# Turning image tokens by 32x32 blocks and transfers inside SBUF in place of TensorE's transposes

## The chip, the cores and the metric

The kernel runs on one core of one Trainium2 chip. A core has TensorE (PE: matrix products, and transposes as a product with a unit matrix), VectorE (DVE), ScalarE (ACT), GpSimd (POOL) and SyncE (SP, which here only issues transfers), with SBUF and PSUM as its memories on chip; 16 DMA engines move data. The metric is device time in microseconds.

## The reference, cut to what matters

The input `x` is an image of 256 channels and 48 x 48 points. Layer 0 normalises it by groups, makes queries, keys and values of 4 heads of 64 and lets all 4 x 2304 = 9216 rows attend to each other; the result, projected, is added to `x`. Layer 1 takes the image as 2304 tokens of 256 channels, adds an attention over 64 learned slices, and then a mixture of 8 experts, of which each token uses two.

```python
qf = q.reshape(B*H*W*nh, dk) / sqrt(dk)          # 9216 x 64
A = softmax(qf @ kf.T, axis=1)                   # 9216 x 9216
x = x + transpose(((A @ vf).reshape(B,H,W,nh*dv)) @ Wo.T + bo)
t = tokens(x)                                    # channels x points  ->  points x channels
h = _ln_t(t) @ W0 + b0                           # normalised over a token's channels
sw = softmax(h @ Ws + bs)                        # 64 slice weights of each token
# slice sums of tokens (weights sw), attention over slices, back to the tokens, then the experts
```

What the change touches is the step `tokens(x)`: the kernel holds `x` with the channels on the partitions, and needs it with the points on the partitions as well.

## The kernel before, in words

Everything is float32. The first 65 us load the image and weights, normalise, and make keys `kk`, queries `q2` and values `v_sb`. The attention of layer 0 then runs to about 1217 us; what follows (the slices' attention, the routing, the experts) ends at 1591.5.

*The attention.* `attention` (L527) runs 18 blocks `b` of 512 queries, two for each group `g` of 256 points (two tiles of 128 points), and in each block 36 pairs of key tiles. For a pair, `scores` makes four products of 64x64 tiles into PSUM (`s`, two buffers), ScalarE takes the exponential into `p` (five buffers), `sums` adds `p` to `acc` on VectorE, and `times_values`, one pair later in TensorE's order, makes four products into `av`, which has one buffer for the whole block. At a block's end `close` (L606) folds `av` into `up` on VectorE; the next block's first `av` product can't start before that has been read.

*The order.* The engines' instructions are recorded through `InOrder` (L52), which keeps them in the written order: each engine works through its own list and waits at its head. TensorE's side work for earlier groups stands at the second pair of a block (`between`, `follow`). The other engines' side work is a list `later`: each piece has a rank, the list is sorted by it (`in_turn`, L417), and one piece is taken from it after the sum of each pair. The ranks give an order and no time.

*The side work.* Group g's blocks are b = 2g and 2g + 1. In block 2g + 3 stands `out_proj` (L421): the output projection into a PSUM bank `pa` and its addition to `x_sb` on VectorE (two pieces). In block 2g + 4 stands `slices` (L439): TensorE transposes the group's four 128x128 pieces of `x_sb` into `pa` and makes the slice and gate logits into `pb`. From `pa` VectorE takes mean and variance of each token (`spread`: `bn_stats`, `bn_aggr`), ScalarE copies the tokens to `t_sb` (`keep`), GpSimd raises the variance to -1/2 (`scales`), and VectorE later writes the normalised tokens `tn` (`norm`). `logits`, `exps`, `gates`, `weights` make the slice weights `sw` from `pb`. In block 2g + 6 stands `gather` (L507): TensorE sums the normalised tokens by slice weights, and VectorE adds the result to `sums_of`. In the last block the side work of groups 6 and 7 that is left is drained in two further steps, each issued once the list before it is empty. The ninth group, g = 8, follows after the attention.

SP issues nothing between the loads at the start and the experts' weights after the attention.

Of the kernel before, what the change touches and what calls it, by code (L numbers as in the profile page):

```python
# [9 lines left out]
FP = mybir.dt.float32  # L10
AF = mybir.ActivationFunctionType
ALU = mybir.AluOpType
# [3 lines left out]
P = 128  # L16
C = 256
# [5 lines left out]
TG = 256  # L23
# [23 lines left out]
def bc(ap, shape):  # L47

    return ap.unsqueeze(2).to_broadcast(shape)
# [16 lines left out]
def layers(  # L66
# [10 lines left out]
    nc = tc.nc  # L77
# [3 lines left out]
    pe, dve, act, pool = (InOrder(tc, e) for e in (nc.tensor, nc.vector, nc.scalar, nc.gpsimd))  # L81
    small = ctx.enter_context(tc.tile_pool(name="small", bufs=2))
# [8 lines left out]
        out=gmat, in_=gmat, pattern=[[-8, 16], [0, 8]], compare_op=ALU.is_ge,  # L91
# [3 lines left out]
        out=gmat, in_=gmat, pattern=[[8, 16], [0, 8]], compare_op=ALU.is_ge,  # L95
        fill=0.0, base=7, channel_multiplier=-1,
    )
    mhalf = const.tile([P, NTT], FP, name="mhalf")
# [11 lines left out]
        out=not_before, in_=not_before, pattern=[[-1, P]], compare_op=ALU.is_ge,  # L110
# [32 lines left out]
    stats = const.tile([P, NTT, 2], FP, name="stats")  # L143
    rstd_t = const.tile([P, NTT], FP, name="rstd_t")
# [10 lines left out]
    t_sb = const.tile([P, NTT, C + E], FP, name="t_sb")  # L155
# [4 lines left out]
    x_sb = l0.tile([P, 2, NT], FP, name="x_sb")  # L160
    for c, pieces in enumerate(((1152, 1152), (1152, 768, 384))):
        at = 0
# [48 lines left out]
    for h in range(H1):  # L211
        at = ((h // 2) % 2 * 2 + h // 4) * D1
        nc.sync.dma_start(
            out=Wout_sb[at : at + D1, h % 2, 0:C], in_=Wout[h * D1 : (h + 1) * D1, :]
# [24 lines left out]
    with proj, tc.tile_pool(name="ps_pj", bufs=5, space=PSUM) as ps_pj, tc.tile_pool(  # L239
        name="ps_spun", bufs=1, space=PSUM  # L240
    ) as ps_spun, tc.tile_pool(
        name="ps_w", bufs=2, space=PSUM
# [49 lines left out]
        for bi, (t0, tn) in enumerate(TBLOCKS):  # L292
            toks = slice(t0, t0 + tn)
# [5 lines left out]
            for m in range(2):  # L299
# [11 lines left out]
                for j in range(2):  # L311
                    rows = slice(j * DK, (j + 1) * DK)
                    at = (2 * m + j) * NT + t0
# [97 lines left out]
    side = layer0.enter_context(tc.tile_pool(name="side", bufs=1))  # L411
    OT = side.tile([P, 2, 2, TG], FP, name="OT")
    tn = side.tile([P, 4, C + 1], FP, name="tn")
    dve.memset(tn[:, :, C : C + 1], 1.0)
    NG = NTT // 2

    def in_turn(work):  # L417
# [3 lines left out]
    def out_proj(g, ps, _):  # L421

        toks = slice(g * TG, (g + 1) * TG)
        for m in range(2):
            for c in range(2):
                pe.matmul(
                    ps[:, m * TG : (m + 1) * TG], WoT[:, c, m * P : (m + 1) * P], OT[:, g % 2, c, :],
                    start=(c == 0), stop=(c == 1),
                )

        def add(m):
            dve.scalar_tensor_tensor(
                x_sb[:, m, toks], ps[:, m * TG : (m + 1) * TG], bcol[:, B_O + m : B_O + m + 1],
                x_sb[:, m, toks], ALU.add, ALU.add,
            )

        return [(2, lambda: add(0)), (3, lambda: add(1))]

    def slices(g, ps, pl):  # L439

        two = range(2 * g, 2 * g + 2)
        for c in range(2):
            for u, i in enumerate(two):
                pe.transpose(
                    ps[:, u * C + c * P : u * C + (c + 1) * P], x_sb[:, c, i * P : (i + 1) * P], ident
                )
        for u, i in enumerate(two):
            at = u * (S + E)
            for c in range(2):
                pe.matmul(  # L450
                    pl[:, at : at + P], x_sb[:, c, i * P : (i + 1) * P],
                    Wl_flat[:, c * (S + E) : c * (S + E) + P], start=(c == 0), stop=(c == 1),
                )
        both = pl[:, 0 : 2 * (S + E)].rearrange("p (u s) -> p u s", u=2)
        lg = small.tile([P, 2, S], FP, name="lg", tag="lg")
        sm = small.tile([P, 2], FP, name="sm", tag="sm")
        nm = small.tile([P, 2], FP, name="nm", tag="nm")
        these = slice(2 * g, 2 * g + 2)

        def keep(u):  # L460
            act.copy(t_sb[:, 2 * g + u, 0:C], ps[:, u * C : (u + 1) * C])

        def spread(u):
            s6 = small.tile([P, 6], FP, name="s6", tag="s6")
            dve.bn_stats(s6, ps[:, u * C : (u + 1) * C])
            dve.bn_aggr(stats[:, 2 * g + u, :], s6)

        def scales():
            ve = small.tile([P, 2], FP, name="ve", tag="ve")
            dve.tensor_scalar(ve, stats[:, these, 1], 1e-5, None, ALU.add)  # L470
            pool.tensor_tensor(rstd_t[:, these], ve, mhalf[:, 0:2], ALU.pow)

        def logits():
            for u, i in enumerate(two):
                dve.scalar_tensor_tensor(
                    lg[:, u, :], both[:, u, 0:S], rstd_t[:, i : i + 1], bl_bc, ALU.mult, ALU.add
                )
            dve.tensor_reduce(nm, lg, AX.X, ALU.max, negate=True)

        def exps():  # L480
            for u in range(2):
                act.activation(
                    lg[:, u, :], lg[:, u, :], AF.Exp, bias=nm[:, u : u + 1], accum_out=sm[:, u : u + 1]
                )

        def gates():
            dve.tensor_copy(t_sb[:, these, C : C + E], both[:, :, S : S + E])

        def weights():
            dve.reciprocal(sm, sm)  # L490
            dve.tensor_tensor(sw[:, these, :], lg, bc(sm, [P, 2, S]), ALU.mult)

        def norm(u):
            i = 2 * g + u
            dve.tensor_scalar(
                tn[:, i % 4, 0:C], t_sb[:, i, 0:C], stats[:, i, 0:1], rstd_t[:, i : i + 1],
                ALU.subtract, ALU.mult,
            )

        at = 9 if g == NG - 1 else 16  # L500
        return [
            (2, lambda: spread(0)), (3, lambda: spread(1)), (4, lambda: keep(0)), (5, lambda: keep(1)),
            (6, scales), (8, logits), (9, exps), (10, gates), (11, weights),
            (at, lambda: norm(0)), (at, lambda: norm(1)),
        ]

    def gather(g, _, pl):  # L507

# [7 lines left out]
        def add():  # L516
            if g == 0:
                dve.tensor_copy(sums_of, new)
            else:
                dve.tensor_tensor(sums_of, sums_of, new, ALU.add)  # L520
            if g == NG - 2:
                dve.tensor_scalar(fold_den, fold[:, 1, :], sums_of[:, C : C + 1], None, ALU.mult)
# [4 lines left out]
    def attention():  # L527


        with tc.tile_pool(name="pexp", bufs=5) as pexp, tc.tile_pool(  # L530
# [104 lines left out]
            def follow(k):  # L635

                pa = ps_side.tile([P, 512], FP, name="pa", tag="pa")
                pb = ps_side.tile([P, 512], FP, name="pb", tag="pb")
                work = []
                steps_of = ((gather, k // 2 - 2), (slices, k // 2 - 1)) if k % 2 else ((out_proj, k // 2 - 1),)  # L640
                for step, g in steps_of:
                    if 0 <= g < NG - 1:
                        work.extend(step(g, pa, pb))
                return work, pa, pb
# [97 lines left out]

    last = NG - 1
    pa = ps_o.tile([P, 512], FP, name="pm", tag="pm")
    for w in in_turn(out_proj(last, pa, None)):
        w()
# [10 lines left out]
    for w in in_turn(slices(last, pa, pb)):  # L757
        w()
# [24 lines left out]
    norm = gating.enter_context(tc.tile_pool(name="norm", bufs=2))  # L783


    with tc.tile_pool(name="sa", bufs=1) as sa, sums_done, tc.tile_pool(
        name="ps_sc", bufs=1, space=PSUM
# [9 lines left out]
        with tc.tile_pool(name="ps_b", bufs=3, space=PSUM) as ps_b:  # L797
# [71 lines left out]
            a = sa.tile([P, 2, 2, S], FP, name="a")  # L869
# [65 lines left out]
        with tc.tile_pool(name="ps_y0", bufs=1, space=PSUM) as ps_y0:  # L935
# [3 lines left out]
            for g, (i0, n) in enumerate(groups):  # L939
                pys = [next(banks)[:, 0 : C + E] for _ in range(n)]  # L940
                for i in range(i0, i0 + n, 4):
                    some = range(i, min(i + 4, i0 + n))
                    for k in some:
                        u = k % 2
# [8 lines left out]
                for k, py in enumerate(pys):  # L953
                    i = i0 + k
                    s6 = small.tile([P, 6], FP, name="s6", tag="s6")
# [7 lines left out]
                these = slice(i0, i0 + n)  # L963
                ve = small.tile([P, n], FP, name="ve6", tag="ve6")
# [5 lines left out]
                    out=t_d[i0 * P : (i0 + n) * P, :].rearrange("(i p) c -> p i c", p=P),  # L970
                    in_=t_sb[:, these, 0:C],
# [12 lines left out]
    with gating, tc.tile_pool(name="onehot", bufs=1) as oh, tc.tile_pool(  # L984
        name="ps_lg", bufs=1, space=PSUM
# [111 lines left out]
        k = 0  # L1097
# [39 lines left out]
    with tc.tile_pool(name="ps_h", bufs=1, space=PSUM) as ps_h, tc.tile_pool(  # L1137
        name="ps_y", bufs=1, space=PSUM
    ) as ps_y, tc.tile_pool(name="ps_t", bufs=1, space=PSUM) as ps_t, tc.tile_pool(
        name="ps_j", bufs=1, space=PSUM  # L1140
# [46 lines left out]
        def turn(xs):  # L1187

            pt = next(ring_pt)
            for c in range(2):  # L1190
                pe.transpose(pt[:, c, :], xs[:, c * P : (c + 1) * P], ident)
            xT = next(ring_xT)
            dve.tensor_copy(xT, pt)
            return xT
# [217 lines left out]
```

## Time and profile before

| | us |
|---|---|
| median of three timed runs (lowest, highest) | 1595.82 (1595.14, 1597.14) |
| the profiled execution, its own time | 1593.33 |
| its span, first to last instruction | 1591.5 |
| TensorE busy in it | 1562.8 |
| VectorE busy | 1029.8 |
| ScalarE busy | 833.8 |
| a block without side work (`up` at 131.42 to `up` at 194.02) | 62.60 |
| a block with a projection (511.87 to 575.75) | 63.88 |
| a block with `gather` and `slices` (447.84 to 511.87) | 64.03 |

The profile is one execution. Its lines read: start, duration, engine, line of the kernel, operation, the tiles written and read, and in square brackets how long the engine had stood idle before it and who released it. Nearly all lines of the source are given as L60, the helper that records them, so one goes by tiles. PEld is TensorE's loading of weights, which runs beside its products. An engine's name with a q is its queue, where transfers are issued. VectorE's operations overlap a little: one of 1.23 us is followed by the next after 1.14.

### The profile page before, as it was taken

What the parts mean: (1) busy time and instruction counts of PE and PEld (TensorE: products, weight loads), DVE (VectorE), ACT (ScalarE), POOL (GpSimd) and SP (SyncE); (2) the same over time, 40 slices, a digit from 0 to 9 for tenths busy, and PEclk for the clock granted to TensorE, in tenths of its full rate; (3) what the DMA queues carried; (4) which work ended last, traced back from release to release, by engine and by line L of the source; (5) the groups of instructions that cost most, each with busy time, mean ns of one, the idle gap of its engine ahead of it and who ended that gap; (6) DMA issues with size and microseconds to landing.
All of it is one profiled execution on the core that took longest, in us unless ns stands there. A gap on an engine that the chain in (4) does not pass through costs nothing. (4 is left out here: it accounts for less than half of the span.)

```text
span 1591.5 us, 31789 instructions
## 1 busy us (share of the span) xinstructions
PE 1562.8 (98%) x13157; PEld 778.2 (49%) x13157; DVE 1029.8 (65%) x1276; ACT 833.8 (52%) x1178; POOL 192.2 (12%) x132
## 2 busy tenths in 40 slices
PE   7999999999999999999999999999999999999998
PEld 3633333333333333333333333333334689999996
DVE  7578787787777877778778778777886721111111
ACT  2366565565565656556556556566654533323231
POOL 0001001011010010110100101101010123433331
PEclk9999999999999999999999999999999999999999
DMA  4000000000000000000000000000000956666665
GB/s 136 1 1 1 1 1 1 1 1 1 1 1 1 2 1 1 1 1 2 1 1 2 1 2 1 1 1 1 2 1 29 329 161 191 176 190 173 191 172 159
DMA packets 38058, 77.43 MB, mean 49 GB/s; under 512 B 3551, under 2 KB 24238, under 8 KB 37774
## 3 DMA queue, kind: packets, MB, share of 16 engines
q1 hardware_dynamic: 30014, 64.65, 12.2%
q0 software_dynamic: 7344, 10.10, 3.8%
q8 instruction: 108, 1.77, 0.5%
q10 hardware_dynamic: 544, 0.52, 0.1%
q14 instruction: 48, 0.39, 0.1%
HBM read 62.94 MB, written 12.32 MB: 47 GB/s over the span
## 5 line engine op out<-in xcount | busy, mean ns | idle before, releaser
L60 DVE TENSOR_TENSOR acc<-acc,p 128x1024 f32<-128x1024 f32 x612 | 749.2, 1224 | 251.3 <-ACT p L60 245.7
L60 ACT ACTIVATE p<-s 128x1024 f32<-128x1024 f32 x648 | 663.4, 1024 | 468.8 <-PE s L60 464.7
L60 PE MATMUL av<-p,v_sb 64*64 64x512 f32 x5184 | 675.1, 590 | 1.8 <-DVE up L60 1.2
L60 PE MATMUL s<-q,kk 64*64 64x512 f32 x5184 | 674.1, 589 | 0.5 <-DVE tn L60 0.5
L60 PEld LDWEIGHTS s<-q,kk 64*64 64x64 f32 x5184 | 200.8, 133 | 354.9 <-issue 181.9
L60 PEld LDWEIGHTS av<-p,v_sb 64*64 64x64 f32 x5184 | 194.6, 131 | 358.1 <-ACT p L60 202.3
L60 ACT ACTIVATE hid<-ph,bcol 128x128 f32<-128x128 f32 x312 | 89.5, 368 | 200.2 <-PE ph L60 199.4
L60 POOL PARTITION_ALL_REDUCE total<-both x17 | 71.2, 4187 | 989.0 <-ACT p L60 810.6
L60 PE MATMUL py<-w_sb,hid 128*128 x624 | 146.9, 379 | 0.0
L60 PEld LDWEIGHTS ph<-xT,w 128*128 128x128 f32 x1248 | 145.2, 192 | 3.4 <-issue 1.6
L60 PE MATMUL ph<-xT,w 128*128 128x128 f32 x1248 | 145.8, 275 | 1.0 <-issue 0.6
L60 DVE COPY xT<-pt 128x256 f32<-128x256 f32 x39 | 16.5, 424 | 161.6 <-PE pt L60 161.6
L60 PEld LDWEIGHTS py<-w_sb,hid 128*128 128x128 f32 x624 | 112.8, 190 | 12.3
L1163 POOL DMA_INDIRECT t_d<-y,slot_t x38 | 60.1, 1582 | 163.4 <-DVE y L60 145.6
L60 DVE TENSOR_TENSOR y<-py,b_bc 128x256 f32<-128x256 f32 x39 | 16.6, 425 | 77.5 <-PE py L60 77.5
L1163 POOL DMA_INDIRECT xs<-tn_d,slot_t x36 | 38.9, 1080 | 15.7 <-issue 10.1
L60 POOL TENSOR_TENSOR rstd_t<-ve,mhalf 128x2 f32<-128x2 f32 (+2 forms) x13 | 11.1, 852 | 171.1 <-DVE ve L60 171.1
L60 DVE RECIPROCAL rinv<-rinv 128x256 f32<-128x256 f32 x17 | 29.7, 1746 | 0.0
L321 DVE TENSOR_SCALAR q<-pp,bcol 64x512 f32<-64x512 f32 (+1 forms) x30 | 20.8, 694 | 7.3 <-PE pp L304 7.0
L60 DVE TENSOR_REDUCE up<-av 128x512 f32<-128x1024 f32 x18 | 22.0, 1224 | 5.0 <-PE av L60 5.0
L60 DVE TENSOR_TENSOR acc<-p 128x1024 f32<-128x1024 f32 x18 | 22.1, 1226 | 4.9 <-ACT p L60 3.3
L60 PE MATMUL spin<-Wqkv_sb,ident 128*128 128x256 f32 x86 | 20.0, 381 | 0.0
(290 smaller groups left out, 597.8 us busy)
## 6 DMA issues: line engine op xcount, KB each, us to landing
w<-in_L_ffn_W_dram SPq DMA_DIRECT2D x39, 1024.0 KB, 6.0
w_sb<-in_L_ffn_W_dram SPq DMA_DIRECT2D x8, 1024.0 KB, 12.0
x_sb<-in_x_dram SPq DMA_DIRECT2D x3, 576.0 KB
t_d<-t_sb SPq DMA_DIRECT2D x2, 768.0 KB
tn_d<-tn SPq DMA_DIRECT2D x2, 768.0 KB
t_sb<-t_d SPq DMA_DIRECT2D x3, 512.0 KB, 5.9
out_dram<-ob SPq DMA_DIRECT2D x3, 512.0 KB
b_bc<-in_L_ffn_b_dram SPq DMA_DIRECT2D x1, 1024.0 KB
```

The source lines that it names most:

```text
L60: return self.tc.keep_in_program_order(getattr(self.engine, name)(*args, **kwargs))
L321: nc.vector.tensor_scalar(dst, pq[rows, 0:tn], bcol[rows, B_Q + m : B_Q + m + 1], 0.125, ALU.add, ALU.mult,)
L1163: new = nc.gpsimd.indirect_dma_start(**kwargs)
```

## The change

For the first eight groups the tokens are no longer turned by TensorE. In the block of the group's projection, after the two additions to `x_sb`, VectorE turns `x_sb` by blocks of 32x32 into a new tile `turned` (`turn`, one instruction of 128x256 for each half of the channels). Each block is then turned in itself, but stands on the partitions of its channels. SP moves the blocks to the partitions of their points, straight into `t_sb` (`move`): for each of the group's two tiles 4 x 4 transfers of 32 partitions with two pieces of 32 numbers each. Mean and variance, `scales` and `norm` follow in the same block, from `t_sb` in place of the PSUM bank. `slices` keeps the logits' products, and transposes for the last group alone. ScalarE's copies `keep` fall away with the transposes. In `later` the order of that block becomes: the two additions, two turns, two moves, `spread` of tile 0, `sides`, `spread` of tile 1, `invert`, `scales`, `divide`, `extremes`, the two `norm`.

```diff
+    turned = side.tile([P, 2, TG], FP, name="turned")
...
+        def turn(m):
+            dve.transpose(turned[:, m, :], x_sb[:, m, toks])
+
+        def move(u):
+            i = 2 * g + u
+            for a in range(4):
+                for k in range(4):
+                    at = u * P + k * 32
+                    nc.sync.dma_start(
+                        out=t_sb[k * 32 : (k + 1) * 32, i, 0:C].rearrange("q (c r) -> q c r", c=2)[
+                            :, :, a * 32 : (a + 1) * 32
+                        ],
+                        in_=turned[a * 32 : (a + 1) * 32, :, at : at + 32],
+                    )
+
+        work = [(2, lambda: add(0)), (3, lambda: add(1))]
+        if g < NG - 1:
+            work += [(4, lambda: turn(0)), (5, lambda: turn(1)), (6, lambda: move(0)), (7, lambda: move(1)), *normed_later(g, 12)]
+        return work
+
+    def normed_later(g, at):
+        these = slice(2 * g, 2 * g + 2)
+        def spread(u, src=None):
+            s6 = small.tile([P, 6], FP, name="s6", tag="s6")
+            dve.bn_stats(s6, t_sb[:, 2 * g + u, 0:C] if src is None else src)
+            dve.bn_aggr(stats[:, 2 * g + u, :], s6)
...
+        return [
+            (at, lambda: spread(0)), (at + 1, lambda: spread(1)), (at + 2, scales),
+            (at + 20, lambda: norm(0)), (at + 21, lambda: norm(1)),
+        ]
...
     def slices(g, ps, pl):
-        for c in range(2):
-            for u, i in enumerate(two):
-                pe.transpose(
-                    ps[:, u * C + c * P : u * C + (c + 1) * P], x_sb[:, c, i * P : (i + 1) * P], ident
-                )
+        if last:
+            for c in range(2):
+                for u, i in enumerate(two):
+                    pe.transpose(
+                        ps[:, u * C + c * P : u * C + (c + 1) * P], x_sb[:, c, i * P : (i + 1) * P], ident
+                    )
...
-        def keep(u):
-            act.copy(t_sb[:, 2 * g + u, 0:C], ps[:, u * C : (u + 1) * C])
...
+        work = [(8, logits), (9, exps), (10, gates), (11, weights)]
+        if last:
+            spread, scales, norm = normed_later(g, 0)
...
```

More of the change, by code (lines that the diff above doesn't have):

```diff
@@ L435, in add @@
             )
-        return [(2, lambda: add(0)), (3, lambda: add(1))]
+        def turn(m):
[11 more added lines that the diff above has]
+                    )
@@ new lines, in out_proj, with scales, norm @@
+        work = [(2, lambda: add(0)), (3, lambda: add(1))]
[8 more added lines that the diff above has]
+            dve.bn_aggr(stats[:, 2 * g + u, :], s6)
+        def scales():
+            ve = small.tile([P, 2], FP, name="ve", tag="ve")
+            dve.tensor_scalar(ve, stats[:, these, 1], 1e-5, None, ALU.add)
+            pool.tensor_tensor(rstd_t[:, these], ve, mhalf[:, 0:2], ALU.pow)
+        def norm(u):
+            i = 2 * g + u
+            dve.tensor_scalar(
+                tn[:, i % 4, 0:C], t_sb[:, i, 0:C], stats[:, i, 0:1], rstd_t[:, i : i + 1],
+                ALU.subtract, ALU.mult,
+            )
+        if g == NG - 1:
+            return spread, scales, norm
+        return [
+            (at, lambda: spread(0)), (at + 1, lambda: spread(1)), (at + 2, scales),
+            (at + 20, lambda: norm(0)), (at + 21, lambda: norm(1)),
+        ]
@@ L439, in slices @@
     def slices(g, ps, pl):
         two = range(2 * g, 2 * g + 2)
-        for c in range(2):
-            for u, i in enumerate(two):
-                pe.transpose(
-                    ps[:, u * C + c * P : u * C + (c + 1) * P], x_sb[:, c, i * P : (i + 1) * P], ident
-                )
+        last = g == NG - 1
+        if last:
[3 more added lines that the diff above has]
+                        ps[:, u * C + c * P : u * C + (c + 1) * P], x_sb[:, c, i * P : (i + 1) * P], ident
+                    )
@@ L458, in slices @@
         these = slice(2 * g, 2 * g + 2)
-        def keep(u):
-            act.copy(t_sb[:, 2 * g + u, 0:C], ps[:, u * C : (u + 1) * C])
[L463 to L471, printed above, removed]
         def logits():
@@ L491, in weights, with keep @@
             dve.tensor_tensor(sw[:, these, :], lg, bc(sm, [P, 2, S]), ALU.mult)
[L493 to L505, printed above, removed]
+        work = [(8, logits), (9, exps), (10, gates), (11, weights)]
+        if last:
+            spread, scales, norm = normed_later(g, 0)
+            def keep(u):
+                act.copy(t_sb[:, 2 * g + u, 0:C], ps[:, u * C : (u + 1) * C])
+            for u in range(2):
+                work += [
+                    (2 + u, lambda u=u: spread(u, ps[:, u * C : (u + 1) * C])),
+                    (4 + u, lambda u=u: keep(u)), (9, lambda u=u: norm(u)),
+                ]
+            work.append((6, scales))
+        return work
     def gather(g, _, pl):
```

## The prediction

> **What bounds the kernel now.** I read the page first (busy time per engine), then the timeline of TensorE and VectorE around two block boundaries, then VectorE's and ScalarE's timeline inside a block, then the waits, then SP's transfers. The page:
>
> ```profile
> PE 1562.8 (98%) x13157; PEld 778.2 (49%) x13157; DVE 1029.8 (65%) x1276; ACT 833.8 (52%) x1178; POOL 192.2 (12%) x132
> ...
> PEclk9999999999999999999999999999999999999999
> DMA  4000000000000000000000000000000956666665
> ```
>
> TensorE is the bound, at full granted clock. The change lives in the attention, from about 69 to 1217 us, where the DMA engines stand still. Inside a block TensorE needs 1.716 us for a pair of key tiles (four score and four value products), VectorE 1.14 us from the start of one sum `acc` to the next operation, ScalarE 1.02 us for one exponential. A block of 36 pairs without side work takes 62.60 us (start of `up` at 131.42 to 194.02); those with side work take 63.9 (511.87 to 575.75) and 64.0 (447.84 to 511.87).
>
> Side work sits at the boundary. TensorE there, in a block with the transposes:
>
> ```profile
> 447.60 1.04 PE L60 MATMUL s<-q,kk 64*64 64x512 f32 x8
> 448.56 0.65 PE L60 MATMUL pb<-tn,sw 128*64 128x257 f32 x4
> 449.15 0.65 PE L60 MATMUL pa<-ident,x_sb 128*128 128x128 f32 x4
> 449.64 1.06 PE L60 MATMUL pb<-Wl,x_sb 128*128 128x128 f32 x8
> 450.63 1.09 PE L60 MATMUL av<-p,v_sb 64*64 64x512 f32 x8
> ```
>
> The four transposes hold TensorE from 449.15 to 449.64, 0.49 us. `av` also needs VectorE's `up`, which ran from 447.84 to 449.06, well before 450.14: that wait doesn't take their place.
>
> VectorE and ScalarE in a block that follows an output projection, where the new work goes:
>
> ```profile
> 521.20 1.21 DVE L60 TENSOR_TENSOR acc<-acc,p 128x1024 f32<-128x1024 f32 x1
> 522.33 0.48 DVE L60 SCALAR_TENSOR_TENSOR x_sb<-pa,bcol,x_sb 128x256 f32<-128x256 f32 x1
> 522.73 1.23 DVE L60 TENSOR_TENSOR acc<-acc,p 128x1024 f32<-128x1024 f32 x1
> 524.62 1.23 DVE L60 TENSOR_TENSOR acc<-acc,p 128x1024 f32<-128x1024 f32 x1 [0.67 <-ACT p L60]
> 525.77 1.75 DVE L60 RECIPROCAL rinv<-rinv 128x256 f32<-128x256 f32 x1
> ```
> ```profile
> 542.28 1.02 ACT L60 ACTIVATE p<-s 128x1024 f32<-128x1024 f32 x1 [0.69 <-PE s L60]
> 543.99 1.02 ACT L60 ACTIVATE p<-s 128x1024 f32<-128x1024 f32 x1 [0.69 <-PE s L60]
> ```
>
> The sum at 524.62 is that of pair 6; the exponential at 543.99 is that of pair 18 (`av` of pair 0 stands at 514.51, one more each 1.716). The waits of the attention show how VectorE can hold the chain at all:
>
> ```profile
> ACT p L60 <- DVE acc L60: 3.5, 5, 0.7
> ```
>
> There are five buffers `p`: the exponential of pair k+5 needs the buffer that the sum of pair k releases. So VectorE may fall about five pairs behind before ScalarE, and then TensorE, waits for it.
>
> SP is idle through the attention. Its transfers of 32 partitions, at the start, are the nearest to the new ones:
>
> ```profile
> L213 SPq DMA_DIRECT2D Wout_sb<-in_L_attn_Wout_dram x8: 311/419/423, 15.4 to 21.5; - x8
> ...
> DMA to landing us min/median/max: 1.6/1.6/1.7
> ```
> ```profile
> 17.08 2.18 SPq L213 DMA_DIRECT2D Wout_sb<-in_L_attn_Wout_dram  x5
> ```
>
> Five in 2.18 us: one each 0.44 us, landing 1.6 us after its issue.
>
> **The change, part by part.** Per group (a pair of token tiles, eight times):
>
> Removed from TensorE: four transposes, 0.49 us each group, all on the path: 8 x 0.49 = -3.9 us. This is all that can be gained. Removed from ScalarE: two copies `t_sb<-pa` of 0.37 us; it waits 0.69 us before each exponential, so nothing.
>
> Added to VectorE: two block transposes of 128x256, not in this trace. Nearest rows: the product `OT` 0.41 us and the `xT` copy 0.42 us, both 128x256; far end the reciprocal of 128x256, 1.75. I take 0.40. The first fills most of the gap of 0.67 us before 524.62; the second ends at 524.62 + 1.14 + 0.40 = 526.16. At 1.75 it would end up to 2.0 us later, and as the chain below starts there, 16 us in all. `bn_stats` and the normalisation move one block earlier, on the same engine; their own time is 0.6 and 0.4 us each, as before. POOL's `rstd_t` moves with them on an idle queue (0.74 us, between reciprocal and normalisation), and `logits` a block later find it done.
>
> Added to SP: 32 transfers of 8 KB a group, 256 in all, 64 pieces of 128 bytes each. They are issued once the second transpose ends, in order, 16 for each tile. Eight semaphores serve them in turn, so each waits for the one eight before; with 8 x 0.44 = 3.5 us against 1.6 to land that is no wait. Issue interval: nearest rows 0.44 (32 rows), 0.47 + 0.05 for loads of 128 partitions at the start, 0.36 to 0.37 + 0.05 for those late in the kernel; ends 0.23 + 0.04 (two rows) and 0.60 + 0.05 (first load of x). I take 0.44. Landing: 1.6 for these, 2.9 for a 256 KB load (`Wv_raw`); I take 1.7.
>
> The wait that this adds stands on VectorE: `bn_stats` of tile 0 waits for 16 transfers after the sum of pair 9, that of tile 1 for all 32 after the sum of pair 11. Behind them on VectorE stand the sums, behind the sums ScalarE's exponentials by their buffers, and behind these TensorE. In the block above:
> - SP starts at 526.3. Tile 0 has landed at 526.3 + 15 x 0.44 + 1.7 = 534.6; the sum of pair 9 would be done at 530.9, so VectorE idles 3.7 us.
> - Sums 10 and 11 run to 537.5. Tile 1 has landed at 526.3 + 31 x 0.44 + 1.7 = 541.6; VectorE idles 4.1 us more. With 0.1 for the wait itself, 541.7.
> - Then `bn_stats` and `bn_aggr` 0.58, sum 12 1.14, the reciprocal 1.66 (start to start), sum 13 1.14: done at 546.2, and with 0.05 the exponential of pair 18 may start at 546.3 in place of 543.99: 2.3 us late. TensorE has about 0.2 us of slack there (0.46 us from the end of an exponential to its `av` here, 0.38 at the closest), so it waits 2.1 us.
> - Afterwards VectorE runs without gaps at 1.14 against 1.716 us a pair. It lags by some 7 us, less than 17 pairs x 0.57 = 9.7, so it has caught up by the next `up`; no further wait.
>
> With interval s and landing l the wait per group is 31s + l - 13.22. At 0.44 and 1.7: 2.1 us, x 8 = 16.9.
>
> Once more in the last block: its side work is drained one step after another, and `gather` of group 7 (TensorE) needs VectorE's `weights` of pair 21. From sum 13 to there VectorE has 8 sums (9.1) and 3.9 of side work (ve 0.2, OT 0.33, extremes 0.92, two norms 0.8, sums and logits 1.05, gates and weights 0.6): 13.0 us. TensorE gets there 8.9 us after the exponential of pair 18 (three pairs 5.15, an exponential 1.03, slack and `av` 1.1, gather and logits of the step before 1.58). It waits 4.1 us, once; before, it waits there 0.1 (`av` from 1188.95 takes 0.86, `gather` starts at 1189.92).
>
> Sum: +16.9 + 4.1 - 3.9 = +17.1 us. The profiled execution took 1593.33 (span 1591.5 and 1.8 around it), 2.5 below the median of the three timed runs; on the median, 1595.8 + 17.1 = 1613.
>
> The row of the 32-row loads shows each started 0.44 us after the last and 1.6 under way, so several were in flight together, and the sum goes by it. A rule speaks worse of the change. The Trainium skill, DMA: Bandwidth & Descriptors, section "Measured (HBM→SBUF, 128 partitions, SWDGE, issued from GpSimd)", gives 0.68 us of transfer for 4 KB, and its rules advise against small transfers; an estimate with 0.68 us for each move, one after another, is 8 x (31 x 0.68 + 1.7 - 13.22) + 0.2 = +77 us, 1672. This trace has no 8 KB transfer to decide it; its 32 KB ones speak against.
>
> **The rivals.**
> A, not slower: the moves land in time. Should SP issue one each 0.37 us or less (landing 1.7), 31s + l is under 13.22 and no exponential is late; the 3.9 us are then set against what is left of the wait in the last block, which is gone at 0.24. Bounds: at 0.27 and 1.6 the last wait is 0.9, so 1593; at 0.37, 1596. For it: the late loads issue in 0.36. Against it: SP leaves some 0.05 between issues, and no row of 32 partitions has less than 0.37 from start to start. The full gain would be 1592.
>
> B, the transfers and not their issue set the pace. A packet of 1 KB takes 50 ns at most (in the slice at 329 GB/s, 16 engines, share 0.9), so a move with four packets on each engine needs 0.2 us, hidden by its issue. If packets of 128 bytes between two places in SBUF took 150 ns, the interval would be 0.6: 8 x (18.6 + 1.7 - 13.22) + 0.2 = +57, 1653. If a move landed only after 4 us, the eight semaphores would make it 0.5: +50, 1646. Against it: nothing else is on the DMA engines then.
>
> C, VectorE itself becomes the bound: no. It is busy 48.7 of 63.9 us in such a block, and gets about 3 us more there while the next block loses as much.
>
> **How the numbers follow.** Forecast, interval 0.38 to 0.53: 1598 to 1635, chance 0.67, own range at the likely ends (0.41 and 1.6; 0.51 and 2.0) 1605 to 1633. A: 0.14, B or a slower issue: 0.19; the far ends of interval and landing together (0.65 and 2.9) give +79, 1675. The range 1594 to 1645 leaves out the best of A and the upper part of B, about 2 in 10. A measurement of this kernel can tell about 0.2%, 3.2 us, from no change: faster than that needs an interval near 0.25 (0.07), within it an interval of up to 0.38 (0.09), slower has the rest, 0.84.
>
> **What the profile after would show.** Right: `bn_stats` of the first eight groups preceded by idle time put down to the transfers `t_sb<-turned`, 3 to 5 us each; `ACT p <- DVE acc` up from 3.5 to some 20 us; blocks after a projection 2 us longer, those after them 0.5 shorter; 256 issues on SP some 0.44 us apart. Wrong: idle under 1 us before `bn_stats` (A), issues well over 0.5 us apart or landings over 3.5 us (B), or a block transpose near 1 us or more.

## The result, and the profile after

The changed kernel takes 1677.35 us (median of six runs, 1671.95 to 1678.87) against 1595.97 before: a ratio of 1.0505, 95% interval 1.0494 to 1.0515. It is 81 us slower; the forecast was 17 us slower, 1613, and the range ended at 1645. The profiled execution took 1677.8, its span is 1676.1.

The page of the changed kernel: TensorE has 21 us more busy time, and the granted clock (`PEclk`: the share of full speed, in tenths) shows dips that it did not have.

```profile
PE 1584.0 (95%) x13125; PEld 776.6 (46%) x13125; DVE 1036.3 (62%) x1292; ACT 828.4 (49%) x1162; POOL 200.5 (12%) x132
...
PEclk9999999999899999999999999999998999999999
```

The waits of the attention (engine and tile that waited, by whom released: us in total, times, longest):

```profile
DVE s L60 <- DMA t_sb<-turned: 120.2, 16, 8.0
...
ACT p L60 <- DVE acc L60: 82.6, 26, 8.7
PE av L60 <- ACT p L60: 64.8, 19, 7.4
```

This is the forecast chain, three links of it in three rows: VectorE waits for the transfers at each of 16 `bn_stats`, ScalarE for VectorE's sums (3.5 us before), TensorE for ScalarE. But each wait of VectorE is 6.7 to 8.0 us, not 3 to 5. One block with a projection, which begins with `up` at 533.35; VectorE:

```profile
560.02 0.43 DVE L60 BATCH_NORM_STATS2 s<-t_sb 128x6 f32<-128x256 f32 x1 [7.72 <-DMA t_sb<-turned]
...
571.06 0.43 DVE L60 BATCH_NORM_STATS2 s<-t_sb 128x6 f32<-128x256 f32 x1 [7.95 <-DMA t_sb<-turned]
...
571.62 1.19 DVE L60 TENSOR_TENSOR acc<-acc,p 128x1024 f32<-128x1024 f32 x1
572.73 1.75 DVE L60 RECIPROCAL rinv<-rinv 128x256 f32<-128x256 f32 x1
574.39 1.16 DVE L60 TENSOR_TENSOR acc<-acc,p 128x1024 f32<-128x1024 f32 x1
```

ScalarE and TensorE in the same stretch:

```profile
572.91 1.02 ACT L60 ACTIVATE p<-s 128x1024 f32<-128x1024 f32 x1 [8.68 <-DVE acc L60]
575.65 1.02 ACT L60 ACTIVATE p<-s 128x1024 f32<-128x1024 f32 x1 [1.72 <-DVE ve L60]
577.60 1.02 ACT L60 ACTIVATE p<-s 128x1024 f32<-128x1024 f32 x1 [0.92 <-PE s L60]
```
```profile
562.95 1.09 PE L60 MATMUL av<-p,v_sb 64*64 64x512 f32 x8 [0.97 <-ACT p L60]
...
573.98 1.98 PE L60 MATMUL av<-p,v_sb 64*64 64x512 f32 x8 [7.37 <-ACT p L60]
575.74 1.77 PE L60 MATMUL s<-q,kk 64*64 64x512 f32 x8
577.35 1.03 PE L60 MATMUL av<-p,v_sb 64*64 64x512 f32 x8
```

The exponential of pair 18 starts at 575.65, when the sum of pair 13 (574.39, 1.16 us) has ended; the row names `ve`, the small operation of VectorE that starts right behind that sum, at 575.47. In the block of before it came 32.12 us after `up` (543.99 - 511.87), here 42.30: 10.2 us late. And the transfers (min, median, max of an issue in ns; then the 32 of this block; then their time to land):

```profile
L446 SPq DMA_DIRECT2D t_sb<-turned x256: 585/595/1681, 271.8 to 1256.3; - x128
L60 DVE STREAM_TRANSPOSE turned<-x_sb x16: 436/437/439, 269.4 to 1234.6; 128x256 f32<-128x256 f32 x16
...
DMA to landing us min/median/max: 1.8/1.8/3.6
```
```profile
547.60 22.11 SPq L446 DMA_DIRECT2D t_sb<-turned  x32
```

SP needs 0.595 us for an issue, and the 32 stand on average (22.11 - 0.595) / 31 = 0.69 us apart: most 0.64, now and then one that takes over 1 us. In the other groups the same sum gives 0.65 to 0.69; the mean of the eight groups is 0.67.

Where the 81 us are, by blocks (start of `up` to start of the next; the last from `up` to the first product on `both` behind the attention):

| | before | after | difference, all |
|---|---|---|---|
| seven blocks with a projection | 63.9 | 73.2 to 75.5, mean 74.0 | +71.0 |
| seven blocks with `slices` | 63.4, then 64.0 | 63.5, then 63.6 | -2.4 |
| the last block | 67.6 | 82.4 | +14.8 |

That makes +83.4 within the attention, of the 84.5 between the two profiled executions.

The wait is not quite all of it. In the seven blocks with a projection the exponential of pair 18 comes 8.9 to 10.2 us late, 9.5 in the mean, and TensorE has some 0.2 us of slack there; but the blocks are 9.3 to 11.6 us longer, 10.1 in the mean. What is left is 0.2 to 1.8 us a block, 0.9 in the mean, 6 us together. It goes with TensorE's clock: the wait is followed by products at half clock (a granted clock of 0.50), for 2.7 us in the block where 0.2 is left, 3.2 to 3.9 where 0.4 to 0.8 is left, and 6.0 where 1.8 is left. This is read from the rows; no run took the clock alone.

### The profile page after: what moved, and what is told of

It reads as the page before. It is cut to its first block, busy times and chain, and to the rows that moved or that the text cites. A ratio compares the mean times of both kernels' runs of the same rounds, so it can differ in the third digit from the quotient of the medians.

```text
span 1676.1 us, 32152 instructions
## 1 busy us (share of the span) xinstructions
PE 1584.0 (95%) x13125; PEld 776.6 (46%) x13125; DVE 1036.3 (62%) x1292; ACT 828.4 (49%) x1162; POOL 200.5 (12%) x132
## 5 line engine op out<-in xcount | busy, mean ns | idle before, releaser
L60 PE MATMUL av<-p,v_sb 64*64 64x512 f32 x5184 | 685.4, 599 | 66.0 <-ACT p L60 64.8
L60 DVE BATCH_NORM_STATS2 s<-t_sb 128x6 f32<-128x256 f32 x19 | 8.1, 428 | 120.3 <-DMA t_sb<-turned 120.2
L60 POOL TENSOR_TENSOR rstd_t<-ve,mhalf 128x2 f32<-128x2 f32 (+2 forms) x13 | 19.3, 1481 | 356.9 <-DVE ve L60 356.9
L1200 POOL DMA_INDIRECT xs<-tn_d,slot_t x36 | 38.8, 1078 | 15.6 <-issue 10.1
```

The costliest lines, as they stand in the source:

```text
L60: return self.tc.keep_in_program_order(getattr(self.engine, name)(*args, **kwargs))
L1200: new = nc.gpsimd.indirect_dma_start(**kwargs)
```

## The experiments

Theory after the result: the chain is as forecast, and the interval between SP's issues was wrong. Rivals: the transfers, their bytes or packets, set the pace; VectorE's added work delays the chain; TensorE's half clock after a long wait is a cost of its own.

**The statistics later.**

```diff
-            work += [..., (6, lambda: move(0)), (7, lambda: move(1)), *normed_later(g, 12)]
+            work += [..., (6, lambda: move(0)), (7, lambda: move(1))]
+            work += [(16, lambda: None)] * 7 + normed_later(g, 17)
```

> The changed kernel with the statistics of the turned tokens taken later: `sides`, `invert`, `divide`, `extremes` come first, then seven empty places in the list, so that `spread` of tile 0 stands after the sum of pair 20 and that of tile 1 after pair 21 (before: 9 and 11). All transfers are made. Theory (SP issues 32 transfers one after another, 0.645 us each, and VectorE's bn_stats waits at the head of its queue for the last, 21.8 us after the second turn; TensorE waits for VectorE through the five buffers): pair 21 comes 14.5 pairs, 25 us, after the turn, so no wait: blocks with a projection back to 63.9 us, blocks with slices 63.6 as measured with the change, the last block without its 14 us: 1595.8 - 6 x 0.4 = 1593, between 1591 and 1595. Rival, VectorE's extra work of 3 us a block or the transfers' traffic delays the chain: the cost stays in good part, over 1610.

Measured: 1593.08 us, against 1595.73 of the kernel before beside it: a ratio of 0.9982, 0.9973 to 0.9990. Blocks with a projection 63.9 us, with `slices` 63.64, the last 67.2 from `up` to `up` (67.5 before). All 256 transfers are made, as slowly as in the change:

```profile
527.08 22.04 SPq L446 DMA_DIRECT2D t_sb<-turned  x32
```
```profile
550.59 0.42 DVE L60 BATCH_NORM_STATS2 s<-t_sb 128x6 f32<-128x256 f32 x1
...
552.31 0.42 DVE L60 BATCH_NORM_STATS2 s<-t_sb 128x6 f32<-128x256 f32 x1
```

No idle time stands before either `bn_stats` (VectorE). The place of the wait is the whole cost, with what follows from TensorE's waiting; neither the traffic nor VectorE's work shows in any block. The attention from the first block with a projection on is 2.6 us shorter than before (959.8 in place of 962.4), which is what leaving out the transposes brings here.

**Without the transfers.**

```diff
-            work += [..., (6, lambda: move(0)), (7, lambda: move(1)), *normed_later(g, 12)]
+            work += [..., *normed_later(g, 12)]
```

> The changed kernel without its 256 transfers: `t_sb` keeps what stood there, so tokens, statistics and routing are other numbers and the stage of the experts may take another time; read by the attention's blocks. Theory: no wait, blocks with a projection 63.9 us in place of 74, blocks with slices 63.6. Rival, VectorE's turns and the earlier statistics delay the chain by themselves: blocks with a projection stay over 66.

Measured: blocks with a projection 63.9, with `slices` 63.65, the attention's end at 1216 us. So VectorE's two turns and the earlier statistics, without the wait, are hidden where the change put them. (The total of 1610.71 us says nothing: other tokens are routed, and the stage of the experts takes longer.)

**Transfers that nothing reads, of eight shapes.** In the kernel before:

```diff
+            for j in range(16):          # spill: a scratch tile, eight places in turn
+                out, in_ = (
+                    (two[:, :, 0:32], x_g[:, :, 0:32]),        # (1) 32 rows x 2 x 128 B
+                    (wide[:, 0:32], x_g[:, 0, 0:32]),          # (2)
+                    (wide[:, 0:64], x_g[:, 0, 0:64]),          # (3)
+                    (two[:, :, 0:128], x_g[:, :, 0:128]),      # (4)
+                    (wide, x_g[:, 0, :]),                      # (5) 32 rows x 1 KB
+                    (wide, Wout[0:32, :]),                     # (6) the same out of HBM
+                    (by_r, x_sb[:, :, g * TG : g * TG + 32]),  # (7) 128 rows
+                    (two[0:2, :, 0:32], x_g[0:2, :, 0:32]),    # (8) 2 rows
+                )[g]
+                nc.sync.dma_start(out=out, in_=in_)
...
+            work.append((6, tries))
```

> The kernel before, and with each of the first eight projections SP issues 16 transfers into a scratch tile that nothing reads, of another shape each time: (1) 32 rows x 2 pieces of 128 B out of SBUF, as in the change; (2) 32 x 1 of 128 B; (3) 32 x 1 of 256 B; (4) 32 x 2 of 512 B; (5) 32 x 1 of 1 KB; (6) 32 rows of 1 KB out of Wout in HBM, as in the row that the prediction used; (7) 128 rows x 2 of 128 B; (8) 2 rows x 2 of 128 B. Theory, issue by SP costs the time and it costs nothing where nobody waits: total as before, 1594 to 1598; (1) 0.645 us from issue to issue; (7), with four times the packets, about the same. What made it 0.645 and not 0.44: the source in SBUF, then (5) 0.6 and (6) 0.44; or the second piece, then (2) and (3) 0.44 and (4) 0.6; or pieces of 128 B, then (1), (2) 0.6 and (3) to (6) 0.44. Rival, the transfers themselves are slow and hold the issue back: (7) two to four times (1), (4) longer than (2) by its eightfold bytes.

Measured: 1597.86 us against 1595.73, a ratio of 1.0012 (1.0002 to 1.0022), with the blocks of the attention as before (63.9 and 64.0); the 2 us are not in the attention, which takes 962.4 us from its first block with a projection on in both. SP's issues, some in a row of each shape; first the three of 32 rows, (1), (5) and (6), then (7) and (8):

```profile
272.48 3.79 SPq L456 DMA_DIRECT2D spill<-x_sb  x6
...
781.67 3.75 SPq L456 DMA_DIRECT2D spill<-x_sb  x6
...
792.88 3.67 SPq L456 DMA_DIRECT2D spill<-in_L_attn_Wout_dram  x8
...
1039.96 2.62 SPq L456 DMA_DIRECT2D spill<-x_sb  x4
...
1167.98 3.29 SPq L456 DMA_DIRECT2D spill<-x_sb  x5
```
```profile
L456 SPq DMA_DIRECT2D spill<-x_sb x112: 507/595/1392, 269.1 to 1174.0; - x112
L456 SPq DMA_DIRECT2D spill<-in_L_attn_Wout_dram x16: 414/419/1724, 788.6 to 797.1; - x16
```

Start to start, (time of the row less one issue) / (count less one): (1) 0.64, (2) 0.63, (3) 0.64, (4) 0.64, (5) 0.63, (7) 0.67, (8) 0.67, and (6) 0.46. Out of SBUF into SBUF an issue costs nearly the same (0.63 to 0.67 from start to start) for 0.5 KB and for 32 KB, for 2 rows and for 128; the same 32 KB out of HBM cost 0.42 us of issue. So neither the second piece nor the 128 bytes made the difference, but the place of the source; and the rival of bytes and packets falls.

**Half the bytes in as many transfers.**

```diff
-                        out=t_sb[k*32:(k+1)*32, i, 0:C].rearrange("q (c r) -> q c r", c=2)[:, :, a*32:(a+1)*32],
-                        in_=turned[a*32:(a+1)*32, :, at : at + 32],
+                        out=t_sb[k*32:(k+1)*32, i, a*32:(a+1)*32],
+                        in_=turned[a*32:(a+1)*32, 0, at : at + 32],
```

> The changed kernel with as many transfers, but each moves one of its two pieces alone (32 x 128 B, the first 128 channels); the other channels of these tokens in `t_sb` are what stood there, so the routing and the experts' time are others; read by the attention's blocks. Theory, SP's time for each issue counts: interval 0.64 as with both pieces, blocks with a projection as with the change, 73 to 75.5 us. Rival, packets or bytes count: the wait for the second tile comes some 8 us earlier, blocks 66 to 68.

Measured: blocks with a projection 70.9 to 73.4, mean 72.5 (74.0 with the change, 63.9 before), `bn_stats` waiting 105 us in place of 120. An issue took 0.589 us in the median. One block, which begins with `up` at 530.91 (VectorE's turns, then SP):

```profile
542.92 0.44 DVE L60 STREAM_TRANSPOSE turned<-x_sb 128x256 f32<-128x256 f32 x1
...
544.70 0.44 DVE L60 STREAM_TRANSPOSE turned<-x_sb 128x256 f32<-128x256 f32 x1
```
```profile
543.38 21.41 SPq L446 DMA_DIRECT2D t_sb<-turned  x32
```

The pace did not change: the mean interval of the seven blocks is 0.67 us, as with the change. What changed is the start. These transfers read the first half of `turned` alone, so SP starts behind the first turn and not behind the second, 12.47 us after `up` in place of 14.25. The exponential of pair 18 comes 7.6 us late in place of 9.5, about as much less; the blocks gain a little less than that, 1.5 of 10.1 us, which is why their mean lies half a microsecond under the range that was expected. So half the bytes and packets saved nothing that shows, and the count of issues sets the pace.

**The wait four sums later.**

```diff
-            work += [..., *normed_later(g, 12)]
+            work += [..., *normed_later(g, 16)]
```

> The changed kernel with `spread` of the two tiles after `sides`, `invert`, `divide` and `extremes`, so after the sums of pairs 13 and 14 in place of 9 and 11; nothing else. The same chain with the issue interval measured since (0.64 us, now and then one of over 1 us, 0.69 in the mean) and 1.8 us to land: on the clock of the block from 511.87 the last transfer lands at 526.16 + 0.1 + 31 x 0.69 + 1.8 = 549.5; 0.1, bn_stats and bn_aggr 0.58, sum 15 1.14: 551.3, and the exponential of pair 20, due at 547.42, waits for it: 3.9 us late, less 0.2 slack. Theory: blocks with a projection 63.9 + 3.7 = 67.6 us (67 to 68.6); the total 7 x 3.7 + 7 in the last block - 2.4 = +31, 1626 (1618 to 1634). Rival, the half clock after a long wait is a cost of its own of some 1.7 us a block: 69.3, 1640. Rival, what counts is the transfers' presence and not the place of the wait: 74, as now.

Measured: 1631.0 us, a ratio of 1.0226 (1.0210 to 1.0241); blocks with a projection 66.9 to 69.9, mean 68.3. Both lie within what was expected, but the mean hides two kinds of blocks. Three take 66.9, 66.9 and 67.3 us, at full granted clock throughout: their exponential of pair 20 comes 3.3 to 3.7 us late, and the block is longer by that less 0.3. The other four, 68.2 to 69.9, each have 3.4 us at half clock, and are 1.4 to 1.6 us longer than the same sum gives. A block of the first kind begins with `up` at 519.71 (VectorE, then TensorE):

```profile
557.08 0.43 DVE L60 BATCH_NORM_STATS2 s<-t_sb 128x6 f32<-128x256 f32 x1 [8.60 <-DMA t_sb<-turned]
```
```profile
560.00 1.09 PE L60 MATMUL av<-p,v_sb 64*64 64x512 f32 x8 [3.09 <-ACT p L60]
```

One of the second kind begins with `up` at 650.64 (TensorE):

```profile
690.21 1.09 PE L60 MATMUL av<-p,v_sb 64*64 64x512 f32 x8 [2.36 <-ACT p L60]
691.12 1.52 PE L60 MATMUL s<-q,kk 64*64 64x512 f32 x8
692.40 1.95 PE L60 MATMUL av<-p,v_sb 64*64 64x512 f32 x8
```

VectorE now waits once a block, 7.9 to 9.6 us, and no longer twice; TensorE waits 2.4 to 4.1 us, in place of 6.2 to 7.4 and up to 1.2 ahead of it, since the wait stands later in the block. So the place of the wait counts, and not the transfers' presence (74); and the half clock is a cost of its own in the four blocks where it came, about as large as the first rival had it (1.7).

**One buffer `p` more.**

```diff
-        with tc.tile_pool(name="pexp", bufs=5) as pexp, ...
+        with tc.tile_pool(name="pexp", bufs=6) as pexp, ...
```

> The changed kernel with six buffers `p` in place of five. Theory: VectorE's wait is the same, but each buffer lets TensorE go on for one more pair, 1.72 us: its two waits of a block together 8.3 - 1.7 = 6.6 us, the total 8 x 1.72 = 13.7 us less, 1663. Half clock after the wait stays, as the wait is still over 5 us at a stretch. Rival, the chain is held by something else than the buffers: no change, 1677.

Measured: 1670.53 us, 6.8 under the change (the kernel before beside them took 1595.73 and 1595.97), where 13.7 were expected. VectorE waits 120.7 us for transfers, as before; blocks with a projection 72.5 to 73.2, mean 72.7, so 1.3 less and not 1.72; the last block gains 0.4. The two profiled executions differ by 9.9 us. The direction tells the buffers from the rival, the size was wrong. ScalarE after the wait, in a block that begins with `up` at 530.08:

```profile
571.64 1.02 ACT L60 ACTIVATE p<-s 128x1024 f32<-128x1024 f32 x1 [1.72 <-DVE ve L60]
573.74 1.03 ACT L60 ACTIVATE p<-s 128x1024 f32<-128x1024 f32 x1 [1.07 <-PE s L60]
576.00 1.03 ACT L60 ACTIVATE p<-s 128x1024 f32<-128x1024 f32 x1 [1.24 <-PE s L60]
```

Two exponentials in a row wait for scores of TensorE, which runs at half clock at that time. Over the seven blocks, the exponential that needs the sum of pair 13 (now that of pair 19) comes 7.9 us late in place of 9.5: the chain did lose about what the buffer was to bring. But what the blocks take beyond it grew from 0.9 to 1.2 us in the mean, so part of the gain went to TensorE's half clock. This too is read from the rows, and no run took the clock alone.

**Copies by ScalarE in place of the transfers.**

```diff
-                    nc.sync.dma_start(out=t_sb[...], in_=turned[...])
+        def move(a, k):                       # both tiles, both halves of the channels
+            act.copy(to[:, :, :, a * 32 : (a + 1) * 32], of[:, :, :, k * 32 : (k + 1) * 32])
...
+            work += [(16, lambda a=a, k=k: (move(a, k), move(a, k + 1))) for a in range(4) for k in (0, 2)]
+            work += normed_later(g, 17)
```

> The changed kernel without transfers: ScalarE copies the turned blocks to the other partitions, 16 copies a group of 32 rows x 128 numbers (both tiles and both halves at once), two after the exponential of each of eight pairs; the statistics follow after pairs 19 and 20. Estimate of a copy from the rows `low<-up` of 64x512, 0.60 us, and `t_sb<-pa` of 128x256, 0.37: some 0.25 to 0.3 us, two of them 0.5 to 0.6 in the 0.69 us that ScalarE waits before an exponential. Theory: hidden, blocks 63.9 and 63.6, total as with late statistics, 1593 (1591 to 1595). Rival, two copies take over 0.7 us and hold the exponentials: up to 8 pairs x 0.3 us a block, 1612.

Measured: 1592.05 us against 1596.18, a ratio of 0.9972 (0.9961 to 0.9983); blocks 63.9 and 63.65. A copy takes 0.295 us, and two fit between two exponentials (ScalarE):

```profile
532.74 1.02 ACT L60 ACTIVATE p<-s 128x1024 f32<-128x1024 f32 x1 [0.69 <-PE s L60]
533.79 0.61 ACT L60 COPY t_sb<-turned 32x128 f32<-32x128 f32 x2
534.46 1.02 ACT L60 ACTIVATE p<-s 128x1024 f32<-128x1024 f32 x1
```

This is the fastest measured here, beside the late statistics; the two were not run on the same chip, and their intervals overlap. In both the attention is 2.5 to 2.6 us shorter than before.

## Why the prediction was wrong

- *TensorE's gain, 8 x 0.49.* Mostly right: 2.5 to 2.6 us in place of 3.9, by the two versions without a wait. The blocks from the second `slices` on are 0.4 us shorter. The logits' products took a little longer without the transposes ahead of them, 608.93 to 610.02 in place of 449.64 to 450.63:

```profile
608.35 0.66 PE L60 MATMUL pb<-tn,sw 128*64 128x257 f32 x4
608.93 1.16 PE L60 MATMUL pb<-Wl,x_sb 128*128 128x128 f32 x8
610.02 1.09 PE L60 MATMUL av<-p,v_sb 64*64 64x512 f32 x8
```

  The first of these blocks gained nothing: its first `av` came 0.4 us earlier, but an exponential later in it (at 343.69) waited 1.11 us for scores in place of the usual 0.69. Why stays open.
- *The turn at 0.40 us.* 0.437; the second ended 14.2 us after `up`, as worked out (14.3).
- *The wait on VectorE, and its way to TensorE.* Right in each link and place: transfers, `bn_stats`, sums, buffers, exponentials, `av`. With what was measured, 0.67 and 1.8, the text's own formula 31s + l - 13.22 gives 9.4 us a block; the exponentials were 9.5 late, 9.3 without the slack. That the 0.69 of the one block shown would give 9.97, nearly the 10.1 of the blocks, is chance: the difference is the half clock.
- *The interval of 0.44 us.* This is the step that failed. The nearest row had the right number of partitions, but came out of HBM; between two places in SBUF an issue takes 0.595 us and the next follows at 0.64, 0.67 in the mean with the long ones. Its 0.23 us, 31 times in each of eight groups, are some 58 of the 66 us by which the attention took longer than forecast (83.4 less 17.1). The far end of the interval was written as 0.65 from the first load of x, but lay outside the range, and a slower issue or slow transfers together had a chance of 0.19; nothing in that trace showed a transfer from SBUF to SBUF.
- *TensorE's clock.* The sum has TensorE at full granted clock, as in the kernel before, and nothing for what a long wait does to it. The half clock made some 6 us in the seven blocks.
- *The landing of 1.7 us.* 1.8.
- *The last block, 4.1 us more.* It took 14.8 us more, about what the longer interval and the 4.1 add up to, but not in the way that was forecast. TensorE did not wait at `gather` (1277.84, without idle time); it waited shortly before, 2.43 us, for an exponential behind ScalarE's exponentials of `lg`, for which ScalarE had waited 3.03 us on VectorE's `nm`. And it ran at half clock for 13.7 us of this block:

```profile
1273.40 1.90 PE L60 MATMUL av<-p,v_sb 64*64 64x512 f32 x8 [2.43 <-ACT p L60]
```

- *Rival B.* Its time was nearer than the forecast's, and its mechanism wrong: with half the packets the pace stayed. The page's 0.68 us for a transfer of 4 KB, by which the estimate came to 1672, came as near by chance. It is a time of transfer, which the estimate put one after another; here the 0.67 is SP's issue, and with 1.8 us to land two to three transfers are in flight together.
- *The range.* 1594 to 1645 held neither the time nor, at its upper end, the case of an interval near 0.65 with a landing near the one measured: 31 x 0.65 + 1.8 - 13.22 = 8.7, x 8 and 0.2 more, is 1666.

## What to carry to other kernels

A price for an issue holds for the pair of memories of its row: for a transfer between two other memories the row is a bound and not a price, and a number that is multiplied by 31 wants its far end in the range with full weight. A wait at the head of a queue that works in order costs what is left after the buffers behind it, so the same slow transfers cost 81 us or nothing by where the wait stands in the list; put what needs them last. Such a wait can cost more than its length: up to 1.8 us a block here, at half clock behind it. Between partitions on chip, 16 small copies by an engine with gaps did what 32 small transfers did, without a landing to wait for.

## What the runs showed that was not expected

SP's issue of a transfer from SBUF to SBUF takes some 0.6 us (0.595 in the median) whatever its size (0.5 to 32 KB, 2 to 128 rows), against 0.42 for 32 KB out of HBM; to HBM out of SBUF the kernel before has 0.36. Why both ends in SBUF cost more stays open, as do the issues of over 1 us now and then (up to 1.68 us in the change; one of the 16 out of HBM took 1.72).

TensorE's clock fell to half around its long waits. Granted clock in two stretches of 5 us of the changed kernel (after the times: busy time of each engine, then clock and DMA share):

```profile
570.00:575.00 5.00, 1.02 (x8) 0.41 (x12) 3.90 (x5) 1.02 (x1) 0.00 (x0) 0.54 0.01 2
575.00:580.00 5.00, 5.00 (x44) 1.53 (x40) 4.97 (x8) 2.73 (x3) 1.76 (x1) 0.78 0.00 0
```

After an idle time of 7.37 us the eight products took 1.98 us in place of 1.04, and full speed came back some 3.3 us after work began (573.98 to 577.35); over the seven blocks it came back after 2.7 to 6.0 us. Read in windows of 0.5 us, the half clock lasts 6.8 us in six of these blocks and 10.2 in one; with the wait four sums later it lasts 3.4 us in four blocks, after waits of 2.36, 3.41, 4.08 and 4.11 us, and does not come in three, after waits of 2.69, 2.71 and 3.09. The Trainium skill, TensorE: Matmul & The Clock Gate, section "What's actually happening", says that the clock is halved after an idle window of about 3.4 us and given back after as long a busy one. The length agrees with these stretches, which are 3.4 us or multiples of it. The condition does not fit every wait: after the one of 2.36 us the clock fell too, about a microsecond after work had begun again (the rows from 690.21 above). How long a wait may be without it is not settled by these runs.
